# A third scatter epoch for the last two blocks, and node results normalised in place

## The chip, the core and the metric

The kernel runs on one core of one Trainium2 chip. The metric is device time in microseconds (us) for one execution; the median of three runs before the change is 1638.09 us (1637.46 to 1638.39). Engines are named as the profile names them: PE (matrix multiply), PEld (its weight loads), DVE (vector), ACT (scalar), POOL (GpSimd, which here issues the indirect DMAs) and SP (which issues most plain DMAs). "PEclk" is the share of full clock that PE was granted.

## What is computed

A graph layer on 6250 nodes and 206,250 edges, then a residual and a layer norm. Cut to what matters:

```python
msg = concat([x[col], edge_attr], 1)          # col = dst, sorted; row = src, random
h = relu(msg @ W1a.T + b1a) @ W1b.T + b1b
agg = segment_sum(h, row) / max(counts, 1)
z = relu(concat([x, agg]) @ W2a.T + b2a) @ W2b.T + b2b
out = layernorm(x + concat([z, x]) @ Wr.T + br)
```

The hard part is the sum over `row`: the edges come in an order that has nothing to do with their target node.

## The kernel before, in words

**Blocks, bins, tiles.** The edges go through in 124 blocks of 13 columns of 128 edges. The target nodes are 49 bins of 128 nodes. For each bin there is a run of slots in DRAM; 128 slots are a *tile* (128 rows of 130 floats, 66.56 KB). For each block the kernel computes the first layer (PE, line 1355; ACT, line 1358), counts on PE and DVE which slot of its bin each edge gets, and POOL scatters the rows, one indirect DMA per column of 128 edges (`scatter`, line 1395). Blocks 4 to 103 also join part of their edges four to a row in a tensor of their own; from block 104 on there are 13 scatters a block and no joins.

**Epochs and steps.** An epoch is a run of blocks with its own slots. A bin's slots are sized for the worst count it may see (`cap` tiles), and at least `low` tiles are surely full; slots between `low` and `cap` are cleared beforehand by DMAs on ACT's queue (`clear`, line 1443, one every second block, twelve and one for each epoch). Before the change there are two epochs, of 114 and 10 blocks. As the edges come in, *steps* read back the tiles that are full by then: a step is a range of tiles for every bin, cut into *groups* of up to three bins. For each group SP loads the tiles (`read`, line 1457, into a ring of nine buffers), DVE turns the node numbers of the rows into a 0/1 matrix `oh` (line 1486), PE multiplies it with the rows (line 1505), and DVE adds the sum to `part` (line 1565). A read of an epoch's last step waits for the scatters of all blocks of that epoch; a read of an earlier step only for the blocks up to its own.

**Order.** PE, ACT, DVE and SP run in the order in which the program is written; POOL's scatters are placed by a scheduler, and those of up to three neighbouring blocks are interleaved there. Three blocks after a step is full its groups are queued; whatever is queued at the end of the 124 blocks is summed in a loop behind them (`while issued or marked`). The second epoch's first step (one tile a bin, full at block 120) is queued at block 123 and is mostly summed in that loop: 16 groups of three tiles.

**The last step.** The last step of the last epoch is fused with the node stage. Before the change it has 17 groups of three bins with three tiles each (147 tiles). In turn `i` of its loop each engine works on several groups at different depths: `means` and `scaled` of group i-1 (DVE lines 1859 and 1860; ACT, line 1866), `turned` of i-2 (PE, line 1873; ACT, line 1875), `layer` of i-3 (PE, line 1879; DVE, line 1880), `residual` of i-4 (PE, line 1886; DVE, line 1888), `squares` of i-5 (ACT, line 1894), `written` of i-6 (ACT, line 1899; DVE lines 1900 and 1902; output DMA on SP, line 1907), and the tile sums of group i. The residual result `y` stands in a ring of three buffers, its normalised copy `normed` in a ring of two, from which the output DMA reads.

Of the kernel before, what the change touches and what calls it, by code (L numbers as in the profile page):

```python
# [8 lines left out]
F32 = mybir.dt.float32  # L9
# [5 lines left out]
ALU = mybir.AluOpType  # L15
# [3 lines left out]
P = 128  # L19
# [430 lines left out]
NG = 13  # L450
WIN = 60
STEP = 43
EPOCHS = (114, 10)
NEAR = 8
HEAD = 117
FULL = ((3, 6, 9, 12, 14), (1,))
BIG = 2.0**20
LATE = 3
BUFS = 2
RD = 6  # L460
SUMS, TILES = 3, 12
SEG = 9
# [2 lines left out]
RING = 8  # L465
# [14 lines left out]
def order_of(ngr):  # L480


    return [i * STEP % ngr for i in range(ngr)]
# [3 lines left out]
def fast_path(  # L487
# [37 lines left out]
    D, N = xT.shape  # L525
# [3 lines left out]
    NB = N // P + 1  # L529
    NGR = NT // NG  # L530
    REM = N - (NB - 1) * P
    NE = len(EPOCHS)
    W = H + 2
    BLK = NG
# [28 lines left out]
    def by_bin(of_bin, of_rest):  # L563
        return [of_bin] * (NB - 1) + [of_rest]
# [9 lines left out]
    def low_of(b, n, first=0):  # L574
        _, mean, dev = edges_of(b, n, first)
        return max(0, int(mean - dev)) // P
# [21 lines left out]
    epochs, at_blk = [], 0  # L598
    for e, n in enumerate(EPOCHS):
        ep_ = Epoch()  # L600
# [13 lines left out]
        ep_.steps, lo = [], by_bin(0, 0)  # L614
        for t in FULL[e]:
            at = next(k for k in range(n) if low_of(0, k, ep_.first) >= t)
# [9 lines left out]
    qep.first, qep.end = JOIN_FROM, JOIN_TO  # L626
    assert JOIN_TO <= EPOCHS[0]

# [16 lines left out]
    NQ = NB * QSTRIDE  # L645
    NREST = P * NJOIN
    for ep_ in epochs:
        ep_.name, ep_.masked, ep_.stride = "", True, None
    qep.name, qep.masked = "q", False

    PADT = max(c - l for ep_ in epochs[:BUFS] for c, l in zip(ep_.cap, ep_.low))
    PADT = max(PADT, max(c - l for c, l in zip(qep.cap, qep.low)))
    STRIDE = max(max(ep_.cap) for ep_ in epochs) * P
    assert NE == BUFS

    const = ctx.enter_context(tc.tile_pool(name="fconst", bufs=1))
    dram = ctx.enter_context(tc.tile_pool(name="fdram", bufs=1, space=DRAM))
    buffers = [dram.tile([NB * STRIDE, W], F32, name=f"rows{i}") for i in range(BUFS)]
    for e, ep_ in enumerate(epochs):
        ep_.rows = buffers[e % BUFS]  # L660
    qep.rows = dram.tile([(NQ + NREST) * QUAD, W], F32, name="quads")
    relt = dram.tile([NGR, NG * P], BF16, name="relt")
    ytab = dram.tile([NB * P, H], F32, name="ytab")
# [66 lines left out]
    hi = ep.tile([P, NT], BF16, name="hi")  # L730
    lo = ep.tile([P, NT], BF16, name="lo")
    rowidx = ep.tile([P, RING * NG], I32, name="rowidx")
# [10 lines left out]
    nc.vector.tensor_copy(mvs[:, :, H:], ident[:, None, WIDE : WIDE + 2].to_broadcast([P, MV, 2]))  # L743
    padrow = const.tile([P, PADT * W], F32, name="padrow")
    nc.gpsimd.memset(padrow, 0.0)
# [4 lines left out]
    with (  # L750
# [173 lines left out]
        state = {"rt": 0, "bad": 3}  # L924
# [38 lines left out]
        nc.vector.memset(even, FULLQUADS)  # L963
        NBAD = 15 + 5 * NE + 2 * sum(map(len, FULL)) + 2 * len(FULLQ)
        bad = const.tile([P, NBAD], F32, name="bad")
# [115 lines left out]
        def places(k, ps):  # L1081


            t = direct(k) + 1
            if joined(k):
                return ps[:, 0, : 2 * HALF * t].rearrange("p (o b t) -> p o b t", o=1, t=t)
            return ps[:, :, : HALF * t].rearrange("p i (b t) -> p i b t", t=t)
# [94 lines left out]
        def slots(k, ps):  # L1182

            ep_ = epoch_of[k]
            c0 = k * BLK
            at = (k - ep_.first) % SEG * BLK
            if at == 0:
                m = min(ep_.end - k, SEG) * BLK
                state["bin"] = slp1.tile([P, SEG * BLK], F32, name="bin_at")[:, :m]
                nc.vector.tensor_scalar(  # L1190
                    state["bin"], hi[:, c0 : c0 + m], float(STRIDE), -BIG, op0=ALU.mult, op1=ALU.add
                )
            j0 = JOIN * joined(k)
            n = BLK - j0
            v = places(k, ps)
            row = slp.tile([P, T], F32, name="row")[:, :n]
            nc.vector.tensor_reduce(
                row, v[:, :, :, :n].rearrange("p i b t -> p t i b"), axis=mybir.AxisListType.XY, op=ALU.max
            )

            def by_now(t):
                nc.vector.tensor_copy(t.rearrange("p (i b) -> p i b", i=v.shape[1]), v[:, :, :, n])

            nc.vector.scalar_tensor_tensor(
                rowidx[:, k % RING * BLK + j0 : (k % RING + 1) * BLK], row, BIG + STRIDE - 1,
                state["bin"][:, at + j0 : at + BLK], op0=ALU.min, op1=ALU.add,
            )
            if k + 1 == EARLY:
                by_now(early)
                wrong(early, epochs[0].low, ALU.is_gt, slp)  # L1210
            for st in ep_.steps[:-1]:
                if k + 1 == st.at:
                    full = slp1.tile([P, 2 * HALF], F32, name="full")
                    by_now(full)
                    wrong(full, st.hi, ALU.is_lt, slp)
            if k + 1 == ep_.end:
                by_now(ep_.tot)
                if (ep_.end - ep_.first) * BLK > 255:
                    most = slp.tile([P, 2 * HALF], F32, name="most")
                    nc.vector.tensor_scalar(  # L1220
                        most, hads[k][:, :, n], 255.5, None, op0=ALU.is_gt, op1=ALU.add,
                        accum_out=bad[:, state["bad"] :][:, :1],
                    )
                    state["bad"] += 1
# [392 lines left out]


        clears = {5 + 2 * i: (0, i) for i in range(CLEAR)}
        for e in range(1, BUFS):  # L1620
            clears.update({EARLY - 23 + 24 * e + 2 * i: (e, i) for i in range(CLEAR)})
        clears.update({6 + 2 * i: (-1, i) for i in range(CLEAR)})
        assert max(clears) < EPOCHS[0] and 5 + 2 * CLEAR <= EARLY

# [59 lines left out]
        counts = counts_of(0, *bins_of(0))  # L1684
        columns(0)
        slots(0, counts)
        for k, ep_ in enumerate(epoch_of):

# [6 lines left out]
            j0 = JOIN * joined(k)  # L1695
# [101 lines left out]
            if k + 1 < NGR:  # L1797
                slots(k + 1, counts)
# [45 lines left out]
        NF = N // P  # L1844
        with tc.tile_pool(name="nw2", bufs=2) as nw2, tc.tile_pool(name="nw", bufs=3) as nw, tc.tile_pool(
            name="nw1", bufs=1
        ) as nw1:

            class Nodes:

# [31 lines left out]
                def residual(self):  # L1882
                    p3 = hp.tile([P, SUMS, D], F32, name="h_ps")
                    for j in range(self.nb):
                        b = slice((self.b0 + j) * P, (self.b0 + j + 1) * P)
                        nc.tensor.matmul(p3[:, j, :], nq[:, b], wzz_t, start=True, stop=True)
                    y = self.y = nw.tile([P, SUMS, D], F32, name="y")
                    nc.vector.tensor_add(y[:, : self.nb, :], p3[:, : self.nb, :], xr[:, self.bins, :])

                def squares(self):  # L1890
# [5 lines left out]
                def written(self):  # L1896
                    n, b0 = self.nb, self.b0
                    rstd = nw.tile([P, SUMS], F32, name="rstd")
                    nc.scalar.activation(rstd[:, :n], self.ssq[:, :n], AF.Sqrt, bias=eps, scale=1.0 / D)
                    nc.vector.reciprocal(rstd[:, :n], rstd[:, :n])  # L1900
                    y = nw2.tile([P, SUMS, D], F32, name="normed")
                    nc.vector.tensor_tensor(
                        y[:, :n, :], self.y[:, :n, :], rstd[:, :n, None].to_broadcast([P, n, D]), op=ALU.mult
                    )
                    full = min(n, NF - b0)
                    if full > 0:
                        nc.sync.dma_start(
                            out[b0 * P : (b0 + full) * P].rearrange("(b p) f -> p b f", p=P), y[:, :full, :]
                        )
                    if full < n:  # L1910
                        nc.sync.dma_start(out[NF * P :], y[:REM, full, :])
# [112 lines left out]
```

## Time and profile before

| | us |
|---|---|
| median of three runs | 1638.09 |
| profiled execution, its own time | 1640.12 |
| its span, first to last instruction | 1638.2 |
| PE busy | 1436.9 (88%) |
| DVE busy | 1359.4 (83%) |
| POOL busy | 1160.3 (71%) |
| ACT busy | 1102.8 (67%) |
| last scatter starts at | 1555.99 |
| sums of the last step run on PE from, to | 1562.99, 1621.3 |

All positions in time are us from the start of the span of the one profiled execution. Busy shares are means over stages with different limits, so a stage is read from its own rows. On PE each product shows as two records, so "x18" on line 1505 is nine tiles. A timeline row gives start, duration, engine, line, operation, result and operands, and in brackets how long the engine had stood idle and what ended that. In DVE rows that follow at once, the start of the next row is the better measure of what one costs, since the end of one overlaps the start of the next.

### The profile page before, as it was taken

To read this page: it belongs to the slowest core of one execution; us is meant where nothing else is said; L and a number is where in the kernel's file an instruction comes from. 1 tells how busy PE (TensorE), PEld (TensorE's weight loads), DVE (VectorE), ACT (ScalarE), POOL (GpSimd) and SP (SyncE) were. 2 spreads that over 40 slices of the span, in tenths; PEclk is the share of its full clock that TensorE was granted. 3 is DMA by queue.
4 is the path that set the end of the run, shared out by engine and by line. 5 is a ranking of instruction groups with operands and counts; after the bars stand their busy time and mean duration, and the time that the engine had idled before them with its cause. 6 is when DMAs were issued, how large, how long until landed. Compare 5 with 4: busy or idle time off the path is not lost.

```text
span 1638.2 us, 33212 instructions
## 1 busy us (share of the span) xinstructions
PE 1436.9 (88%) x10881; PEld 1306.3 (80%) x10881; DVE 1359.4 (83%) x3176; ACT 1102.8 (67%) x2247; POOL 1160.3 (71%) x1250
## 2 busy tenths in 40 slices
PE   6688888989999999999999999999986998799587
PEld 5577777778888888888888888888876998798476
DVE  7598888887888888999999999999966886776476
ACT  3289999987877777778878788877852344332044
POOL 6777777777777777777777777777776777777700
PEclk9699999999999999999999999999988999999788
DMA  8768888887887988677677667676879999897472
GB/s 208 218 227 288 289 285 293 293 262 240 251 259 227 269 237 246 203 231 216 202 222 217 216 204 235 199 227 194 237 229 342 324 324 290 265 280 241 132 207 78
DMA packets 230179, 393.44 MB, mean 240 GB/s; under 512 B 43205, under 2 KB 164935, under 8 KB 229743
## 3 DMA queue, kind: packets, MB, share of 16 engines
q1 hardware_dynamic: 155629, 224.57, 48.4%
q0 software_dynamic: 48240, 121.28, 21.0%
q10 hardware_dynamic: 26130, 45.38, 7.9%
q8 instruction: 89, 1.46, 0.4%
q14 instruction: 91, 0.75, 0.1%
HBM read 217.82 MB, written 173.25 MB: 239 GB/s over the span
## 4 chain that ended last, share of the span: by engine, by line
PE 55%; ACT 15%; DMA 14%; DVE 8%; issue 4%; POOL 2%; ACTq 1%; SPq 0%; DVEq 0%; POOLq 0%
PE h_ps L1505 23%; PE h_ps L1267 11%; DMA rows<-orow,rowidx 9%; PE h_ps L1355 9%; PE h_ps L1280 5%; ACT rhs L1320 4%; ACT rj L1272 3%; ACT orow L1283 2%; POOL rows L1395 2%; DMA rt<-rows 2%; DVE marks L1235 1%; ACT orow L1358 1%; ACT marks L1240 1%; ACT rhs L1318 1%; PE cnt_ps L1094 1%
## 5 line engine op out<-in xcount | busy, mean ns | idle before, releaser
L1395 POOL DMA_INDIRECT rows<-orow,rowidx x985 | 952.6, 967 | 329.8 <-issue 174.1
L1505 PE MATMUL h_ps<-rt,oh 128*128 128x129 f32 x4036 | 504.0, 280 | 43.8 <-DVE oh L1486 39.4
L1505 PEld LDWEIGHTS h_ps<-rt,oh 128*128 128x128 f32 x4036 | 479.3, 195 | 46.5 <-issue 40.8
L1486 DVE TENSOR_TENSOR oh<-ramp,rt 128x768 f32<-128x768 bf16 (+2 forms) x427 | 317.8, 779 | 46.0 <-DMA rt<-rows 42.3
L1267 PE MATMUL h_ps<-marks,side 128*128 128x512 f32 x1254 | 317.3, 402 | 2.8 <-ACT xr_now L1655 2.2
L1355 PE MATMUL h_ps<-mv,rhs 124*128 124x128 f32 x1970 | 278.3, 287 | 31.6 <-ACT orow L1358 31.5
L1280 PE MATMUL h_ps<-mv,rj 128*128 128x130 f32 x1672 | 234.1, 286 | 72.4 <-ACT orow L1283 45.5
L1280 PEld LDWEIGHTS h_ps<-mv,rj 128*128 128x128 f32 x1672 | 212.8, 193 | 106.2 <-ACT orow L1283 57.6
L1355 PEld LDWEIGHTS h_ps<-mv,rhs 124*128 124x128 f32 x1970 | 249.6, 198 | 35.8 <-ACT orow L1358 33.4
L1267 PEld LDWEIGHTS h_ps<-marks,side 128*128 128x128 f32 x1254 | 229.7, 190 | 48.3 <-ACT xr_now L1655 3.5
L1235 DVE TENSOR_TENSOR marks<-quad_ramp,ramp 128x1024 fp32r<-128x1024 f32 x209 | 250.6, 1203 | 0.0
L1366 POOL DMA_INDIRECT quads<-orow,qidx x209 | 202.3, 968 | 66.1 <-issue 18.4
L1358 ACT ACTIVATE orow<-h_ps 128x384 f32<-128x384 f32 (+1 forms) x287 | 151.4, 536 | 143.5 <-PE h_ps L1355 138.0
L1272 ACT COPY rj<-h_ps 128x512 f32<-128x512 f32 x209 | 119.7, 588 | 77.4 <-PE h_ps L1267 76.8
L1565 DVE TENSOR_TENSOR part<-part,h_ps 128x387 f32<-128x387 f32 (+2 forms) x232 | 113.1, 488 | 68.4 <-PE h_ps L1505 67.6
L1241 ACT ACTIVATE marks<-marks,ones 128x512 fp32r<-128x512 f32 x209 | 150.9, 722 | 6.8
L1283 ACT ACTIVATE orow<-h_ps 128x260 f32<-128x260 f32 x418 | 139.8, 389 | 23.3 <-PE h_ps L1280 19.4
L1240 ACT ACTIVATE marks<-quad_ramp,z_act 128x512 fp32r<-128x512 f32 x209 | 149.4, 715 | 0.0
L1052 DVE TENSOR_TENSOR_SCAN had<-ramp,bins 128x400 bf16<-128x400 bf16 (+1 forms) x124 | 135.0, 1089 | 17.1 <-ACT bins L1073 4.5
L1318 ACT ACTIVATE rhs<-rhs,from_win 60x896 f32<-60x896 bf16 (+1 forms) x116 | 130.5, 1125 | 2.9
L1320 ACT ACTIVATE rhs<-rhs,ones 60x896 f32<-60x896 f32 (+1 forms) x116 | 130.2, 1122 | 2.9
L1346 ACT CAST orow<-lo 128x7 f32<-128x7 bf16 (+1 forms) x124 | 24.2, 195 | 150.9 <-DMA rows<-orow,rowidx 139.1
(189 smaller groups left out, 1471.9 us busy)
## 6 DMA issues: line engine op xcount, KB each, us to landing
rt<-rows SPq DMA_DIRECT2D x145, 390.0 KB
rt<-quads SPq DMA_DIRECT2D x98, 390.0 KB
rhs<-in_edgeT SPq DMA_DIRECT2D x91, 224.0 KB
rt<-rows SPq DMA_DIRECT2D x98, 195.0 KB
enat<-in_edgeJ SPq DMA_DIRECT2D x91, 192.0 KB
rows<-orow,rowidx POOLq DMA_INDIRECT x985
rows<-padrow ACTq DMA_DIRECT2D x12, 1300.0 KB
quads<-padrow ACTq DMA_DIRECT2D x11, 1300.0 KB
```

What stands on the lines that cost most here:

```text
L1235: nc.vector.tensor_tensor(m[:, :n, :], all_q[:, None, :].to_broadcast([P, n, QUAD * P]), z[:, :n, None].to_broadcast([P, n, QUAD * P]), op ...
L1267: nc.tensor.matmul(ps, s[:, p, i * JOIN + t, :], m[:, t, :], start=t + p == 0, stop=t == JOIN - 1 and p == 1,)
L1272: nc.scalar.copy(rj, ps)
L1280: done[k, f"join{i}"] = nc.tensor.matmul(ps[:, j, :], rj[:, (g0 + j) * P : (g0 + j + 1) * P], m, start=True, stop=True).ins.name
L1283: nc.scalar.activation(mrow[:, g0 : g0 + 2, :], ps, AF.Relu)
L1320: nc.scalar.activation(rhs[D:WIDE, :], rhs[D:WIDE, :], AF.Relu, bias=ones[D:WIDE, :1], scale=-1.0)
L1355: done[k, c] = nc.tensor.matmul(ps[:, j, :], rhs[:WIDE, of * P : (of + 1) * P], m[:WIDE, :H], start=True, stop=True).ins.name
L1358: nc.scalar.activation(orow_of(k, k0, n)[:, :, :H], ps[:, :n, :], AF.Relu)
L1366: s = nc.gpsimd.indirect_dma_start(out=qep.rows.rearrange("(q r) f -> q (r f)", r=QUAD), out_offset=bass.IndirectOffsetOnAxis(ap=qidx[:, q ...
L1395: s = nc.gpsimd.indirect_dma_start(out=ep_.rows, out_offset=bass.IndirectOffsetOnAxis(ap=rowidx[:, k % RING * BLK + j : k % RING * BLK + j ...
L1486: nc.vector.tensor_tensor(res[:, at_tile : at_tile + nb * n, :], ramp[:, None, :].to_broadcast([P, nb * n, P]), node[:, :, None].to_broadc ...
L1505: m = nc.tensor.matmul(of_bin(b), oh[:, at_tile, :], rt[:, j * n + t, : H + 1], start=t0 + t == st.lo[b], stop=t0 + t == st.hi[b] - 1,)
```

## The change

Three epochs of 114, 8 and 2 blocks take the place of 114 and 10. Each has its own DRAM tensor and its own number of slots per bin (`ep_.stride`: 2560, 512 and 256 rows; before, 2560 for both). The second epoch's caps are 3 or 4 tiles a bin and the third's 1 or 2. Its clears (twelve and one) come at blocks 55 to 77. In the node stage the normalised result is written over `y`, and `y` has five buffers where `y` and `normed` had three and two.

```diff
-EPOCHS = (114, 10)
+EPOCHS = (114, 8, 2)
-FULL = ((3, 6, 9, 12, 14), (1,))
+FULL = ((3, 6, 9, 12, 14), (1,), ())
...
-        ep_.name, ep_.masked, ep_.stride = "", True, None
+        ep_.name, ep_.masked, ep_.stride = "", True, max(ep_.cap) * P
...
-    STRIDE = max(max(ep_.cap) for ep_ in epochs) * P
-    assert NE == BUFS
...
-    buffers = [dram.tile([NB * STRIDE, W], F32, name=f"rows{i}") for i in range(BUFS)]
     for e, ep_ in enumerate(epochs):
-        ep_.rows = buffers[e % BUFS]
+        ep_.rows = dram.tile([NB * ep_.stride, W], F32, name=f"rows{e}")
...
-        for e in range(1, BUFS):
+        for e in range(1, NE):
             clears.update({EARLY - 23 + 24 * e + 2 * i: (e, i) for i in range(CLEAR)})
...
-                    y = self.y = nw.tile([P, SUMS, D], F32, name="y")
+                    y = self.y = nw5.tile([P, SUMS, D], F32, name="y")
...
-                    y = nw2.tile([P, SUMS, D], F32, name="normed")
+                    y = self.y
                     nc.vector.tensor_tensor(
-                        y[:, :n, :], self.y[:, :n, :], rstd[:, :n, None].to_broadcast([P, n, D]), op=ALU.mult
+                        y[:, :n, :], y[:, :n, :], rstd[:, :n, None].to_broadcast([P, n, D]), op=ALU.mult
                     )
```

What it moves, on SP, behind the 16 reads of the second epoch's first step. In these rows `rows_65` is the second epoch's tensor, `rows_66` the third's, and "128x3x260" is three bins of two tiles. Before, the first rows of the last step, which reads three tiles a bin, in pairs of a two-bin and a one-bin read:

```order
L1457 DMA rt<-rows_65 128x3x130 x16
L1457 DMA rt<-rows_65 128x2x390
L1457 DMA rt<-rows_65 128x390
L1457 DMA rt<-rows_65 128x2x390
L1457 DMA rt<-rows_65 128x390
```

After, from the same place, the first and the last rows of what stands there:

```order
L1453 DMA rt<-rows_65 128x3x130 x16
L1453 DMA rt<-rows_65 128x3x260 x3
L1453 DMA rt<-rows_65 128x2x260
L1453 DMA rt<-rows_65 128x390
L1453 DMA rt<-rows_65 128x260
```

```order
L1453 DMA rt<-rows_65 128x2x260
L1453 DMA rt<-rows_65 128x390
L1453 DMA rt<-rows_66 128x3x130 x5
L1453 DMA rt<-rows_66 128x260
L1453 DMA rt<-rows_66 128x2x130
```

The second epoch's rest is now a step of its own, 17 groups in 27 reads with 106 tiles, summed in the loop behind the blocks; the node stage follows with the third epoch's 17 groups in 19 reads with 51 tiles.

On POOL, the end of the scatters. Buffers `orow_141` and `orow_142` hold the rows of blocks 120 and 121, `orow_143` and `orow_144` those of blocks 122 and 123. The order is that of before, where all of them went to `rows_65`; after, the last rows read:

```order
L1391 DMA rows_65<-orow_141,rowidx 25088x130
L1391 DMA rows_66<-orow_143,rowidx 12544x130 x3
L1391 DMA rows_66<-orow_144,rowidx 12544x130 x2
L1391 DMA rows_65<-orow_142,rowidx 25088x130
L1391 DMA rows_66<-orow_143,rowidx 12544x130
L1391 DMA rows_66<-orow_144,rowidx 12544x130
L1391 DMA rows_65<-orow_142,rowidx 25088x130 x2
L1391 DMA rows_66<-orow_143,rowidx 12544x130
L1391 DMA rows_66<-orow_144,rowidx 12544x130
L1391 DMA rows_65<-orow_142,rowidx 25088x130
L1391 DMA rows_66<-orow_144,rowidx 12544x130 x7
```

Behind these stand four more to `rows_66`. The last scatter of the second epoch is thus the twelfth from the end.

On DVE, one turn of the node stage's loop, before:

```order
L1565 TENSOR_TENSOR part<-part,h_ps 128x387
L1859 TENSOR_SCALAR rc<-part 128x3
L1860 RECIPROCAL rc<-rc 128x3
L1900 RECIPROCAL rstd<-rstd 128x3
L1902 TENSOR_TENSOR normed<-y,rstd 128x192
L1888 TENSOR_TENSOR y<-h_ps,xr 128x192
L1880 TENSOR_TENSOR x_late<-x_late,h_ps 128x384
L1486 TENSOR_TENSOR oh<-ramp,rt 128x768
L1486 TENSOR_TENSOR oh<-ramp,rt 128x384
```

After:

```order
L1561 TENSOR_TENSOR part<-part,h_ps 128x387
L1855 TENSOR_SCALAR rc<-part 128x3
L1856 RECIPROCAL rc<-rc 128x3
L1896 RECIPROCAL rstd<-rstd 128x3
L1898 TENSOR_TENSOR y<-y,rstd 128x192
L1884 TENSOR_TENSOR y<-h_ps,xr 128x192
L1876 TENSOR_TENSOR x_late<-x_late,h_ps 128x384
L1482 TENSOR_TENSOR oh<-ramp,rt 128x384
```

One of the two `oh` rows has gone from the turn, and the normalisation writes to what it reads. PE's tile sums in a turn go from nine tiles to three.

More of the change, by code (lines that the diff above doesn't have):

```diff
@@ L452 @@
 STEP = 43
-EPOCHS = (114, 10)
+EPOCHS = (114, 8, 2)
 NEAR = 8
 HEAD = 117
-FULL = ((3, 6, 9, 12, 14), (1,))
+FULL = ((3, 6, 9, 12, 14), (1,), ())
 BIG = 2.0**20
 LATE = 3
-BUFS = 2
 RD = 6
@@ L647, in fast_path @@
     for ep_ in epochs:
-        ep_.name, ep_.masked, ep_.stride = "", True, None
+        ep_.name, ep_.masked, ep_.stride = "", True, max(ep_.cap) * P
     qep.name, qep.masked = "q", False
-    PADT = max(c - l for ep_ in epochs[:BUFS] for c, l in zip(ep_.cap, ep_.low))
+    PADT = max(c - l for ep_ in epochs for c, l in zip(ep_.cap, ep_.low))
     PADT = max(PADT, max(c - l for c, l in zip(qep.cap, qep.low)))
-    STRIDE = max(max(ep_.cap) for ep_ in epochs) * P
-    assert NE == BUFS
     const = ctx.enter_context(tc.tile_pool(name="fconst", bufs=1))
     dram = ctx.enter_context(tc.tile_pool(name="fdram", bufs=1, space=DRAM))
-    buffers = [dram.tile([NB * STRIDE, W], F32, name=f"rows{i}") for i in range(BUFS)]
     for e, ep_ in enumerate(epochs):
-        ep_.rows = buffers[e % BUFS]
+        ep_.rows = dram.tile([NB * ep_.stride, W], F32, name=f"rows{e}")
     qep.rows = dram.tile([(NQ + NREST) * QUAD, W], F32, name="quads")
@@ L1190, in slots @@
                 nc.vector.tensor_scalar(
-                    state["bin"], hi[:, c0 : c0 + m], float(STRIDE), -BIG, op0=ALU.mult, op1=ALU.add
+                    state["bin"], hi[:, c0 : c0 + m], float(ep_.stride), -BIG, op0=ALU.mult, op1=ALU.add
                 )
@@ L1204, in slots @@
             nc.vector.scalar_tensor_tensor(
-                rowidx[:, k % RING * BLK + j0 : (k % RING + 1) * BLK], row, BIG + STRIDE - 1,
+                rowidx[:, k % RING * BLK + j0 : (k % RING + 1) * BLK], row, BIG + ep_.stride - 1,
                 state["bin"][:, at + j0 : at + BLK], op0=ALU.min, op1=ALU.add,
@@ L1846, in fast_path @@
             name="nw1", bufs=1
-        ) as nw1:
+        ) as nw1, tc.tile_pool(name="nw5", bufs=5) as nw5:
             class Nodes:
```

## Prediction

> **What bounds the kernel now.** The change leaves the first 114 blocks alone but for some clears, so I read the end first: the busy time by stage, from the windows view (columns: PE, PEld, DVE, ACT, POOL busy with counts, PEclk, DMA share, GB/s).
>
> ```profile
> span 1638.2 us, 33212 instructions
> 1520.00:1560.00 40.00, 16.02 (x118) 13.88 (x116) 15.25 (x33) 0.00 (x0) 28.10 (x30) 0.75 0.38 107
> 1580.00:1600.00 20.00, 20.00 (x163) 18.43 (x162) 18.32 (x49) 14.47 (x66) 0.00 (x0) 1.00 0.63 175
> 1598.66:1609.60 10.94, 10.94 (x89) 10.00 (x89) 10.12 (x28) 6.77 (x34) 0.00 (x0) 1.00 0.59 161
> ```
>
> From 1520 to 1560 PE is busy for 16 of 40 us while POOL works through the last scatters; from 1580 on PE is never idle. So there is a hole ahead of the node stage, and a node stage that PE bounds. The chain that ended last says where the hole ends and what one turn of the node stage costs (start, us, what):
>
> ```profile
> 1542.11 2.44 DMA rows<-orow,rowidx
> ...
> 1555.99 2.29 DMA rows<-orow,rowidx
> ...
> 1558.46 3.38 DMA rt<-rows
> ...
> 1561.93 0.97 DVE oh L1486
> ...
> 1562.99 4.22 PE h_ps L1505 x18
> ...
> 1587.69 2.01 PE h_ps L1505 x18
> 1589.70 0.61 PE h_ps L1886 x6
> 1590.32 0.70 PE h_ps L1879 x2
> 1591.02 0.33 PE h_ps L1873 x3
> ...
> 1616.94 2.02 PE h_ps L1505 x18
> ```
>
> The last scatter lands at 1558.3, the last step's first read needs 3.5 us until DVE can start, and the first nine tiles are summed at 1567.21. A turn takes PE 2.01 + 0.61 + 0.70 + 0.33 = 3.65 us, of which nine tiles take 2.01, 0.223 each. The sixteenth group is summed at 1618.96, so fifteen turns take 51.75 us.
>
> **The change, part by part.**
>
> *The rest of the second epoch (106 tiles) moves into the hole.* It may start when its own last scatter has landed. By POOL's order that is the twelfth scatter from the end. POOL issues one every 1.262 us ((1555.99 - 1542.11) / 11), so it is the one of the chain's first row, down at 1544.55: the reads get 14 us of the hole, not all of it. As before, DVE starts some 3.5 us after that, at 1548.0. What the 17 groups cost DVE stands in the timeline of the preceding sums:
>
> ```profile
> 1505.22 1.81 DVE L1486 TENSOR_TENSOR oh<-ramp,rt 128x768 f32<-128x768 bf16 x2
> ...
> 1533.36 0.55 DVE L1565 TENSOR_TENSOR part<-part,h_ps 128x387 f32<-128x387 f32 x1
> 1533.82 0.55 DVE L1486 TENSOR_TENSOR oh<-ramp,rt 128x384 f32<-128x384 bf16 x1
> 1534.29 0.55 DVE L1565 TENSOR_TENSOR part<-part,h_ps 128x387 f32<-128x387 f32 x1
> ...
> 1535.22 1.69 DVE L1565 TENSOR_TENSOR part<-part,h_ps 128x387 f32<-128x387 f32 x3
> ```
>
> An add costs 0.46 and an `oh` of three tiles 0.47 from start to start, one of six tiles 0.905; a straight line gives 0.147 a tile and 0.025 a read. So 106 x 0.147 + 27 x 0.025 + 17 x 0.46 = 24.1 us on DVE. PE's 106 x 0.223 = 23.7 us lie beside it. But PE has stood still from 1536 on and starts cold: before, its first nine tiles took 4.22 us instead of 2.01 (the chain), in a window with PEclk 0.58 (the second row of the next fence), so 2.2 us more. The Trainium skill, "TensorE: Matmul & The Clock Gate", Part 1, states that a PE idle for some 3.4 us falls to half clock and needs about 3.4 busy us to come back. By that the loss is an estimated 1.7 us, and the sum 0.5 us shorter; the row shows a longer loss, and I take the row. Behind the last `oh` come the last sum and its add, 0.67 + 0.46 us. The rest is done at 1548.0 + 24.1 + 2.2 + 1.1 = 1575.4.
>
> Can the reads keep up? From the DMA view, 1518 to 1528 and 1562 to 1568 (packets, MB, share):
>
> ```profile
> 1516.00:1530.00 14.00, 13.85 (x113) 12.88 (x112) 10.46 (x23) 0.00 (x0) 10.64 (x12) 1.00 0.95 254
> 1562.00:1568.00 6.00, 5.01 (x27) 5.04 (x28) 3.50 (x6) 0.00 (x0) 0.00 (x0) 0.58 1.03 360
> q1 hardware_dynamic: 3977, 1.98, 78.1%
> rt<-rows SPq DMA_DIRECT2D x11, 195.0 KB
> ...
> q1 hardware_dynamic: 1494, 2.16, 102.9%
> ```
>
> Reads of one tile a bin (packets of 520 bytes) take 0.781 x 16 x 10 us / 3977 = 31 ns a packet, those of three tiles 66 ns. The rest has two tiles a bin, between them: about 49 ns, so 106 tiles in 53 x 128 packets keep 16 engines for 20.8 us. That is under DVE's 24.1, so DMA costs nothing here; if that cover is gone, see the second rival. The same 1516 row has POOL at its pace (12 scatters in 14 us) beside a busy DVE and 95% DMA, so the last scatters do not slip.
>
> *The third epoch's first group.* Its rows have long landed by 1575.4. One `oh` (0.47) and three tiles (0.67) put the first sum at 1576.5, against 1567.21: **+9.3 us**.
>
> *The turns of the node stage.* They lose six tiles on PE (3.65 - 1.34 = 2.32 us left, with three tiles at 0.67) and one `oh` on DVE. One turn on DVE:
>
> ```profile
> 1615.33 0.56 DVE L1565 TENSOR_TENSOR part<-part,h_ps 128x387 f32<-128x387 f32 x1 [0.17 <-PE h_ps L1505]
> 1615.92 0.17 DVE L1859 TENSOR_SCALAR rc<-part 128x3 f32<-128x3 f32 x1
> 1616.13 0.18 DVE L1860 RECIPROCAL rc<-rc 128x3 f32<-128x3 f32 x1
> 1616.22 0.15 DVE L1900 RECIPROCAL rstd<-rstd 128x3 f32<-128x3 f32 x1
> 1616.40 0.36 DVE L1902 TENSOR_TENSOR normed<-y,rstd 128x192 f32<-128x192 f32 x1
> 1616.68 0.35 DVE L1888 TENSOR_TENSOR y<-h_ps,xr 128x192 f32<-128x192 f32 x1
> 1616.94 0.55 DVE L1880 TENSOR_TENSOR x_late<-x_late,h_ps 128x384 f32<-128x384 f32 x1
> 1617.41 0.55 DVE L1486 TENSOR_TENSOR oh<-ramp,rt 128x384 f32<-128x384 bf16 x1
> ...
> 1581.22 1.28 ACT L1899 ACT_TABLE_LOAD   x1
> ```
>
> From 1615.33 to 1617.41 are 2.08 us, and the `oh` adds 0.47: 2.55 us a turn. ACT has 6.77 us in the three turns from 1598.66, 2.26 each. So **DVE takes PE's place as the bound**, at 2.55 us. The first turns have less: two without `x_late`, `y`, `rstd` and `normed` (1.36 each by the same starts), one with `x_late` (1.83), two with `y` too (2.09 each), then ten full ones; and ACT's table load, hidden before in a turn of 3.65 us, falls in a turn of 2.1 and is counted in full, 1.28. Together 2.72 + 1.83 + 4.18 + 25.5 + 1.28 = 35.5 us against 51.75: **-16.2 us**. Bounds for the turn: 2.32 (PE's) and 3.65 (as before); 2.55 is the sum of rows that follow at once.
>
> *Five buffers, in place.* The multiplication reads and writes the same shapes, so it costs its 0.28 us still. It no longer waits for an output to land, which it does twice at the end:
>
> ```profile
> 1629.26 0.36 DVE L1902 TENSOR_TENSOR normed<-y,rstd 128x192 f32<-128x192 f32 x1 [0.21 <-DMA out_dram<-normed]
> ...
> 1631.83 0.36 DVE L1902 TENSOR_TENSOR normed<-y,rstd 128x192 f32<-128x192 f32 x1 [2.13 <-DMA out_dram<-normed]
> ```
>
> Both lie on the path: **-2.3 us**. The wait moves to the writer of `y`, three turns after the output is issued, 7.6 us at 2.55. The chain has the wait for an output at
>
> ```profile
> 1628.24 3.50 DMA out_dram<-normed
> ```
>
> 3.5 us, so nothing is late there.
>
> *Clears.* Thirteen more DMAs on ACT's queue at blocks 55 to 77, and smaller ones for the second epoch.
>
> ```profile
> L1443 ACTq DMA_DIRECT2D rows<-padrow x26: 338/366/672, 87.5 to 629.4; - x26
> 480.00:800.00 320.00, 299.05 (x2295) 271.26 (x2294) 285.49 (x690) 254.40 (x505) 235.25 (x245) 1.00 0.77 231
> ```
>
> An issue takes ACT 0.366 us: 0 to 4.8 us in all. There ACT is busy for 254 of 320 us and PE, at 299, is nearer to being the bound, so I take **+1.0**. The added DVE rows at blocks 120 to 123 (a memset, a copy, a check) fall where DVE waits for PE: nothing.
>
> *Sum:* 9.3 - 16.2 - 2.3 + 1.0 = -8.2 us. The profiled execution took 1640.12 (its span and 1.9 us around it) and would take 1631.9; the median of the runs lies 2.0 lower, so 1638.09 - 8.2 = **1629.9**.
>
> **The rivals.**
>
> 1. *The rest waits for the last scatter of all.* If its reads are let go only at 1558.4 and not at 1544.6, all that follows is 13.8 us later: 1643.7, slower than before. The point from which it decides: a start after 1552.8 eats the gain, one after 1556 makes it slower by more than 0.2%. For it: before, the last step's first read follows the last scatter in the chain. Against it: the second epoch's one-tile reads landed (11 of them from 1518 to 1528) while scatters to the same tensor went on.
>
> 2. *The rest is bound by its reads.* Those 11 reads moved 198 GB/s beside the scatters, 0.336 us a tile. At that rate 106 tiles take 35.6 us instead of the 26 that DVE and the cold PE need, some 9 us more: 1639. For it: 95% DMA share in that window. Against it: packets twice as long, and no scatters after 1558. The Trainium skill, "DMA: Bandwidth & Descriptors", "Why small descriptors are slow (HBM only)", gives a fixed overhead of about three cycles a packet, which makes two-tile packets hardly dearer per byte than three-tile ones and speaks against this rival; the two rows above (31 and 66 ns for a third and all of the bytes) show a larger one.
>
> 3. *The turns do not reach DVE's sum.* With the engines nearly level (2.55, 2.32, 2.26) each waits for the other; at 3.0 us a turn the ten full turns give back 4.5 us, and the shorter ones 1.5: 1636.
>
> 4. *The rest starts earlier,* at 1527, if all of blocks 120 and 121 were scattered ahead of 122. Some 14 us better: 1616. POOL's order speaks against it.
>
> **How the numbers follow.** Forecast 1629.9 (0.70; its own range 1623 to 1636, from 2 to 3 us either way in the rest's start and pace, 1.5 in the turns, 0 to 4.8 in the clears); rival 1: 0.06; rival 2: 0.12; rival 3: 0.07; rival 4: 0.05. The range 1623 to 1640 takes in rivals 2 and 3. A measurement of this kernel can tell about 0.2% (3.3 us) from no change. Faster by more than that is below 1634.8: nearly all of the forecast, rival 4 and a part of rival 3, 0.77. Slower is above 1641.4: rival 1, 0.06. Between: 0.17.
>
> **What would show it.** The first `rt` read of the rest issued near 1544.6, in step with the twelfth scatter from the end; DVE without idle from 1548 to 1575; the first three-tile sum of the node stage near 1576; turns of 2.55 us with PE waiting for `oh` or for DVE's results; no output DMA named as releaser of the normalisation; and positions up to block 113 within some 2 us of before. Wrong would be: reads released with the last scatter (rival 1), DVE waiting for `rt` throughout the rest (rival 2), turns near 3 us (rival 3), or the blocks' own pace changed by more than the clears can explain.

## The result, and the profile after

The changed kernel takes 1633.93 us (median of 12 runs, 1630.50 to 1640.22) against 1640.88 us for the kernel before (12 runs, 1637.41 to 1644.56): a ratio of 0.9961, 95% interval 0.9946 to 0.9976, so 6.4 us (2.5 to either side) faster. Its profiled execution took 1632.16 us, its span is 1630.3.

The windows of the changed kernel (columns as before: PE, PEld, DVE, ACT, POOL busy with counts, PEclk, DMA share, GB/s):

```profile
span 1630.3 us, 33371 instructions
1520.00:1560.00 40.00, 26.38 (x193) 24.27 (x192) 26.46 (x52) 0.00 (x0) 25.35 (x27) 0.83 0.69 206
1544.00:1574.00 30.00, 26.84 (x220) 26.71 (x221) 26.29 (x48) 0.00 (x0) 7.14 (x8) 0.89 0.96 298
1580.00:1600.00 20.00, 19.27 (x134) 16.35 (x133) 17.41 (x56) 16.72 (x75) 0.00 (x0) 0.97 0.35 85
```

From 1520 to 1560 PE is busy for 26 us instead of 16: the hole is partly filled. From 1580 on PE has pauses where it had none. The timeline shows what starts the filling:

```profile
1538.43 0.96 POOL L1391 DMA_INDIRECT rows<-orow,rowidx  x1 [0.30 <-DMA rows<-orow,rowidx]
...
1540.92 43.09 SPq L1453 DMA_DIRECT2D rt<-rows  x41
...
1545.21 0.96 DVE L1482 TENSOR_TENSOR oh<-ramp,rt 128x768 f32<-128x768 bf16 x1 [12.81 <-DMA rt<-rows]
...
1546.27 25.92 PE L1501 MATMUL h_ps<-rt,oh 128*128 128x129 f32 x212 [13.33 <-DVE oh L1482]
...
1552.32 0.96 POOL L1391 DMA_INDIRECT rows<-orow,rowidx  x1 [0.30 <-issue]
```

The first row is the twelfth scatter from the end. SP issues the rest's first read 2.5 us behind its start, DVE takes it up 4.3 us later, and PE needs 25.9 us for the 106 tiles (212 records), most of it behind the last scatter. Then the chain (start, us, what) shows the node stage:

```profile
1573.08 0.92 PE h_ps L1501 x6
...
1589.61 0.48 DVE part L1561
...
1592.14 0.48 DVE part L1561
...
1594.67 0.47 DVE part L1561
...
1612.30 0.51 DVE part L1561
...
1623.29 0.23 DVE y L1898
```

The adds to `part` stand 2.53 us apart and lie on the chain: DVE sets the turn. Since whole executions differ by 3 or 4 us whatever the kernel, I compare all traces by their distance from the start of their last scatter (us; "first rc" is DVE's first `rc` of the node stage, 0.6 behind its first sum):

| kernel (chip) | rest's first `oh` | first rc | 16th rc | last normalisation ends | span ends |
|---|---|---|---|---|---|
| before | | 11.84 | 63.59 | 76.54 | 82.21 |
| after | -7.11 | 22.30 | 60.52 | 71.20 | 77.98 |
| e8_before (8) | | 16.27 | 68.02 | 81.30 | 87.32 |
| e2_buffers (8) | | 16.24 | 67.99 | 78.68 | 85.98 |
| e1_epochs (8) | | 38.25 | 74.83 | 87.67 | 93.50 |
| e4_wait_last (8) | | 38.37 | 76.61 | 87.30 | 93.91 |
| e9_after (14) | | 39.15 | 75.75 | 86.44 | 93.35 |
| e6_warm (14) | | 39.79 | 77.08 | 87.77 | 94.05 |
| e5_order (14) | | 47.45 | 84.06 | 94.75 | 101.29 |
| g1_order (13) | | 45.62 | 82.23 | 92.93 | 100.08 |
| f1_light_before (6) | | 11.96 | 63.80 | 75.93 | |
| f2_light_after (6) | -12.44 | 16.58 | 53.16 | 63.87 | |
| f3_light_order (6) | | 7.43 | 44.01 | 54.70 | |
| g2_order (6) | -18.32 | 9.53 | 46.11 | 56.80 | 63.11 |

So the tail shrank by 82.21 - 77.98 = 4.2 us. The other 3.7 us between the two spans are a last scatter that came at 1552.32 instead of 1555.99; the experiments ask whether that is the change's.

The chips matter here: on chip 6 and in the measurement above, whose chip isn't known, the kernel before takes 1638 to 1641 us at a mean granted clock near 0.96; on chips 8, 13 and 14 it takes 2118 to 2151 us at 0.87. Ratios are always to the kernel before on the same chip.

### The profile page after: what moved, and what is told of

The parts are those of the page before. It is cut to its first block, busy times and chain, and to the rows that moved or that the text cites. A ratio compares the mean times of both kernels' runs of the same rounds, so it can differ in the third digit from the quotient of the medians.

```text
span 1630.3 us, 33371 instructions
## 1 busy us (share of the span) xinstructions
PE 1442.6 (88%) x10901; PEld 1309.7 (80%) x10901; DVE 1369.7 (84%) x3210; ACT 1103.3 (68%) x2246; POOL 1160.6 (71%) x1268
## 4 chain that ended last, share of the span: by engine, by line
PE 56%; ACT 17%; DMA 12%; DVE 8%; issue 4%; POOL 2%; SPq 0%; ACTq 0%; DVEq 0%; POOLq 0%
PE h_ps L1501 24%; PE h_ps L1263 11%; PE h_ps L1351 9%; DMA rows<-orow,rowidx 8%; PE h_ps L1276 5%; ACT rhs L1316 4%; ACT rj L1268 3%; ACT orow L1279 2%; POOL rows L1391 2%; DMA rt<-rows 2%; ACT orow L1354 2%; ACT marks L1236 2%; ACT rhs L1314 1%; DVE marks L1231 1%; PE cnt_ps L1090 1%
## 5 line engine op out<-in xcount | busy, mean ns | idle before, releaser
L1482 DVE TENSOR_TENSOR oh<-ramp,rt 128x768 f32<-128x768 bf16 (+3 forms) x440 | 321.3, 763 | 30.5 <-DMA rt<-rows 27.0
L1561 DVE TENSOR_TENSOR part<-part,h_ps 128x387 f32<-128x387 f32 (+2 forms) x249 | 122.2, 491 | 66.8 <-PE h_ps L1501 65.3
```

Of the source, the lines that this page charges most:

```text
L1482: nc.vector.tensor_tensor(res[:, at_tile : at_tile + nb * n, :], ramp[:, None, :].to_broadcast([P, nb * n, P]), node[:, :, None].to_broadc ...
```

## The experiments

**The parts alone, and the start of the rest.** Epochs without the new rings:

```diff
-                    y = self.y = nw5.tile([P, SUMS, D], F32, name="y")
+                    y = self.y = nw.tile([P, SUMS, D], F32, name="y")
...
-                    y = self.y
+                    y = nw2.tile([P, SUMS, D], F32, name="normed")
```

> The three epochs alone, with the old rings (y of three, normed of two). Theory A (the rest of the second epoch fills the scatter hole and the node stage becomes DVE-bound; the buffers only clear the drain): the turns stay at 2.53 us and the sixteenth sum of the node stage stays where the change has it (some 60 us after the start of the last scatter), while the drain behind it goes back from 11.0 to 13.3 us, with an output DMA named as releaser; 2.3 us slower than the whole change, so some 4 us (0.25%) faster than before. Rival B (the buffers carry most of the gain): about as slow as before, with waits for outputs inside the turns, near 3 us each.

The rings without the epochs (the same lines the other way round, in the kernel before):

> The five in-place buffers alone, with two epochs. Theory A: turns stay at 3.65 us and PE-bound, the first sum of the node stage stays 11.2 us behind the start of the last scatter, the drain takes 11.0 us instead of 13.3: 2.3 us (0.14%) faster than before. Rival B: faster by 5 us or more. For the 3.5 us that the changed kernel was ahead from 57 us on: if the third tensor and its addresses cause it, the blocks start here where they start in before; if it is chance, anywhere within some 4 us of both.

The whole change with a later start of the rest:

```diff
+            if st is epochs[1].steps[-1]:
+                of += [t for j in (122, 123) for t in range(j * BLK, (j + 1) * BLK)]
             for t in of:
```

> The whole change, but the reads of the rest of the second epoch also wait for the scatters of blocks 122 and 123. Theory A (the gain hangs on when the rest may start): the first of these reads goes out with the last scatter's landing, 13.9 us later than in the changed kernel, and all behind it is later by as much, less what a wholly idle DMA gives back (up to 1 us): tail from the last scatter's start 91 us instead of 78, so some 13 us slower than the changed kernel and 6 us (0.4%) slower than before. Rival (the node stage's faster turns are worth having wherever the rest stands): no slower than before.

And the kernel before, unchanged:

> The kernel before once more, for a second profile of its blocks. If the 3.5 us by which the changed kernel's blocks ran ahead are chance of one execution, its blocks start at places that differ from the first profile by as much as 2 to 4 us, and the lead stems from the same transfers near 40 to 57 us; if they are the change's, the blocks start where they did, within 0.5 us.

Measured on chip 8: e1_epochs 2126.22 us, ratio 1.0058 (1.0022 to 1.0093); e2_buffers 2118.55, 1.0006 (0.9972 to 1.0040); e4_wait_last 2132.98, 1.0077 (1.0034 to 1.0120); e8_before 2123.58 in its one run. **The epochs alone are slower than before here**, which neither theory had: turns are 2.53 us as expected, but the first rc stands at 38 instead of 22, and e4's extra wait changes nothing (first rc 38.37 against 38.25). The reason is in e8_before already. PE's largest wait (us in total, times, longest), and PE's rows ahead of the last scatter at 2034.48:

```profile
PE h_ps L1505 <- issue: 129.4, 140, 7.5
```

```profile
2018.26 1.07 PE L1505 MATMUL h_ps<-rt,oh 128*128 128x129 f32 x3 [1.03 <-issue]
2020.36 0.37 PE L1505 MATMUL h_ps<-rt,oh 128*128 128x129 f32 x1 [1.03 <-issue]
2021.06 0.38 PE L1505 MATMUL h_ps<-rt,oh 128*128 128x129 f32 x1 [0.32 <-issue]
2022.46 0.38 PE L1505 MATMUL h_ps<-rt,oh 128*128 128x129 f32 x1 [1.02 <-issue]
...
2030.19 16.12 PE L1505 MATMUL h_ps<-rt,oh 128*128 128x129 f32 x100 [0.60 <-issue]
```

PE stands still again and again with nothing that the trace names ("issue"; why it does, no run shows), and is still summing the second epoch's first step when the last scatter is out. There is no hole: the rest is queued behind those sums, so its 24 us come on top whenever it is let go. That is why e4 can't price rival 1 here; on a chip with a hole it wasn't tried. What the two kernels have in common with the first pair still shows: in e1_epochs the drain waits for an output as before,

```profile
2116.68 0.36 DVE L1898 TENSOR_TENSOR normed<-y,rstd 128x192 f32<-128x192 f32 x1 [2.09 <-DMA out_dram<-normed]
```

and nowhere else, and from the 16th rc to the last normalisation it takes 12.8 us against 10.7 in e2_buffers (13.3 in e8_before). So rival B, that the buffers carry the gain, falls: they touch the drain alone.

**The changed kernel beside the kernel before, idle products, another order of the scatters.** Three kernels on chip 14. The changed kernel once more:

> The changed kernel once more, beside the kernel before on the same chip. Theory A with its condition (the change pays only if PE has done with the sums of the second epoch's first step before that epoch's last scatter lands): on a chip with a granted clock near 0.96, 0.2 to 0.6% faster than before, the tail behind the last scatter's start 78 us against 82; on one near 0.87, where the tail of the three epochs alone took 93.5 us against 87.3, 91 us against 87 and so 0.1 to 0.3% slower. Rival (the gain came from a start that was 3.5 us ahead in the first 60 us): on either chip the same ratio.

Products that nobody reads in the first four turns:

```diff
                 if i < n_last:
                     on_way.append(Nodes(sum_next(NGR)))
+                if i < 4:
+                    for _ in range(3):
+                        nc.tensor.matmul(cnt[:, 1, :P], ident, ident, start=True, stop=True)
```

> The whole change with three idle products of 128x128 (0.22 us each, into a bank that nobody reads) behind the sums of the first four turns of the node stage. If the half clock of the fourth turn (PEclk 0.50 from 1578 to 1580, the layer's product 1.65 us instead of 0.86) comes from PE standing still for much of 1572 to 1578, the clock stays at 1.00 and the turn takes 2.4 us instead of 4.2: 1 to 2 us faster than the changed kernel. Rival (the clock falls there for another reason): turns as before, up to 1 us slower for the added products.

The scatters of the last four blocks without the waits that interleave them:

```diff
+            if k >= 120:
+                pace = {}
             for j in range(j0, BLK):
```

> The whole change, but the scatters of blocks 120 to 123 no longer wait for the products of later blocks, so that POOL's order puts all 26 scatters of blocks 120 and 121 ahead of the 26 of blocks 122 and 123: the last scatter of the second epoch is the twenty-seventh from the end instead of the twelfth. Theory A (the rest's start sets the gain): where PE is granted nearly full clock, the first reads of the rest follow at once behind those of the second epoch's first step, about 5 us earlier than in the changed kernel, DVE and PE go on without a pause and without the half clock, and the first sum of the node stage stands some 9 us behind the start of the last scatter instead of 21: 8 to 13 us faster than the changed kernel. Rival (the rest is bound by its reads beside the scatters, 0.336 us a tile): the rest takes 36 us and the gain is 3 us at most. On a chip with the lower clock (0.87) the sums of the second epoch's first step end behind the last scatter anyway, so there it should change nothing.

Measured: e9_after 2160.93 us, ratio 1.0060 (1.0029 to 1.0090); e6_warm 2156.27, 1.0008 (0.9972 to 1.0044); e5_order 2158.34, 1.0031 (0.9996 to 1.0067). The whole change is slower than before on such a chip, by more than I expected. By the table, e9_after's tail is 6.0 us longer than that of e8_before, on another chip (93.35 against 87.32): its first rc comes 22.9 us later, its turns and drain give back 17.7, its end costs 0.9. The interval, 6 to 19 us, may hold more than that; what else there is stays open. That rest, on a PE that comes to it warm:

```profile
2095.25 23.91 PE L1501 MATMUL h_ps<-rt,oh 128*128 128x129 f32 x212 [0.42 <-PE h_ps L1501]
```

```profile
2090.00:2120.00 30.00, 28.62 (x244) 27.48 (x242) 29.45 (x58) 0.00 (x0) 0.00 (x0) 1.00 0.92 277
```

DVE is busy for 29.45 of 30 us. The new order of scatters doesn't help here, as expected; its distances from the last scatter are longer, as that scatter no longer waits for PE and goes out earlier relative to it.

e6 went at one row of the first profile. In what follows a turn is counted by the rc that ends it, so the fourth turn lies between the third rc and the fourth. After's PE in its first turns, and the stretches at half clock in after and in e4_wait_last (granted clock: third number from the end):

```profile
1575.55 0.91 PE L1869 MATMUL h_ps<-ident,agg 128*128 128x128 f32 x3 [0.89 <-ACT agg L1862]
1576.30 0.84 PE L1501 MATMUL h_ps<-rt,oh 128*128 128x129 f32 x6
1577.75 1.65 PE L1875 MATMUL h_ps<-aT,wam_t 128*128 128x384 f32 x2 [0.61 <-ACT aT L1871]
1579.19 0.84 PE L1869 MATMUL h_ps<-ident,agg 128*128 128x128 f32 x3
1579.84 1.48 PE L1501 MATMUL h_ps<-rt,oh 128*128 128x129 f32 x6
```

```profile
1577.75:1581.16 3.41, 3.41 (x12) 2.69 (x13) 1.37 (x4) 1.46 (x4) 0.00 (x0) 0.50 0.16 39
```

```profile
2063.05:2066.46 3.41, 3.41 (x15) 2.85 (x14) 1.51 (x4) 1.46 (x4) 0.00 (x0) 0.50 0.13 34
```

PE runs at half clock for 3.4 us though it had not stood still for more than 0.9 us since the rest began; the fourth turn takes 4.24 us. In e4_wait_last it takes 3.97 and the fifth 0.3 too long, in the other seven kernels with three epochs and without the idle products the fourth takes 2.59 to 2.60. So it strikes by chance, in two of nine executions, and costs 1.65 us both times (38.2 us from the first rc to the 16th, against 36.6). With the idle products the clock stayed at 1.00, but in one execution that shows little; they also cost 0.7 us in the fifth turn (3.12 against 2.44). Whether they prevent the half clock stays open. The Trainium skill, "TensorE: Matmul & The Clock Gate", Part 1, has the clock set by PE's activity in a free-running window of some 3.4 us. The 3.41 us of each stretch agree with that, and so does that the same instructions meet it in one execution and not in the next. Its rule of one idle window alone doesn't give the fall: PE was busy for 3.17 of the 5.50 us from 1572.20 on, with no idle time above 0.9 us.

**PE put in time by leaving out products.** To get the hole back on whatever chip, three kernels multiply only the first tile of each bin in late steps:

```diff
                     for t in range(n):
+                        light = st.at >= 104 and st.epoch in (qep, epochs[0])
+                        if light and t0 + t != st.lo[b]:
+                            at_tile += 1
+                            continue
...
-                            start=t0 + t == st.lo[b], stop=t0 + t == st.hi[b] - 1,
+                            start=t0 + t == st.lo[b], stop=light or t0 + t == st.hi[b] - 1,
```

With these products missing, the program goes on into its general path behind the node stage (6.9 ms in all), so only positions up to the last normalisation are read.

> The kernel before, relieved on PE: of the steps that are full at block 104 or later in the first epoch and among the joined rows, only the first tile of each bin is multiplied (some 650 products fewer in blocks 108 to 122, so its output isn't the reference's; reads, DVE's matrices and scatters stay). Its use is to put PE in time for the end of the scatters on a chip whose PE is slow. Expected: PE waits for the last scatter again, the first sum of the node stage ends some 11 us behind its start as in the first profile (16.3 without the relief here), and the tail from its start takes 81 to 83 us.

> The changed kernel with the same relief (the same products left out). Theory A (the change pays when PE has done with the first step of the second epoch before that epoch's last scatter lands, and costs when not): the reads of the rest go out 11 to 12 us ahead of the last scatter's start again, instead of 2 to 4 us behind it, the first rc of the node stage stands at 22 us instead of 38 to 39, and the tail takes 76 to 78 us, 4 to 6 us less than that of the relieved kernel before. Rival (this chip's transfers or engines, not PE's lateness, make the change slower here): the tail stays at 90 us or more, longer than that of the relieved kernel before.

> The changed kernel with the same relief, and with the scatters of blocks 120 and 121 all ahead of those of 122 and 123. Theory A (with PE in time, the rest's start sets the gain): the reads of the rest follow the twenty-seventh scatter from the end, some 30 us ahead of the last one's start, the rest is summed before the last scatter lands, the first rc of the node stage stands 9 to 11 us behind the last scatter's start, and the tail takes 64 to 67 us, 10 to 13 us less than with the old order. Rival (the reads beside the scatters are so slow, 0.336 us a tile, that the early start is lost): first rc at 14 us or later, or scatters stretched from their 1.26 us.

They came to chip 6, where PE isn't late even without the relief. Windows from 1540 to 1560 of f1_light_before, then of f2_light_after, then of f3_light_order (and its 20 us ahead):

```profile
1540.00:1560.00 20.00, 0.00 (x0) 0.00 (x0) 0.00 (x0) 0.00 (x0) 11.79 (x13) 0.50 0.22 66
```

```profile
1540.00:1560.00 20.00, 16.12 (x130) 16.15 (x131) 16.10 (x29) 0.00 (x0) 12.45 (x13) 0.82 1.00 320
```

```profile
1520.00:1540.00 20.00, 19.08 (x144) 16.89 (x143) 19.80 (x40) 0.00 (x0) 15.12 (x17) 1.00 1.00 314
1540.00:1560.00 20.00, 16.88 (x147) 16.36 (x146) 16.68 (x32) 0.00 (x0) 11.83 (x13) 1.00 0.78 249
```

In f1 PE and DVE do nothing at all in the hole; its last normalisation ends at 75.93, as in the kernel before (76.54). In f2 the work starts inside the hole, and it ends at 63.87, 12.1 us sooner than f1; the full kernel gained 5.3 to the same point (76.54 - 71.20), and I had expected 4 to 6. Between the two changed kernels, 71.20 and 63.87, lie 7.3 us, and two things make them. The products left out also move POOL's order: here the last scatter of the second epoch is the sixteenth from the end, not the twelfth, so its reads go out 5.0 us sooner (4 x 1.262). The first `oh` stands at -12.44 instead of -7.11, 5.3 sooner, and the first rc at 16.58 instead of 22.30, 5.7 sooner: **the start of the rest passes through to the node stage, nearly us for us.** And the half clock didn't strike (1.65). In f3 the rest is done when the last scatter lands; first rc at 7.43, end at 54.70. The rival with slow reads falls: the first rc is well ahead of its 14 us, and at a DMA share of 1.00 POOL kept its 1.26 us a scatter. No run on chips 8, 13 or 14 took PE's lateness away, so that this lateness makes the change slower there is read from their traces, not shown by an experiment.

**The new order, nothing left out.** The kernel of e5_order ran on two more chips.

> The kernel with the scatters of blocks 120 and 121 ahead of those of 122 and 123 and nothing left out, once more. Theory A, for a chip on which PE is granted about 0.96 (on one with 0.87 it repeats what was seen there): PE ends the second epoch's first step some 19 us ahead of the last scatter's start, the rest follows without a pause, DVE needs 24 us for it, so the first rc of the node stage stands 7.5 to 10 us behind the last scatter's start (22.3 in the changed kernel, 7.4 in the relieved kernel with this order), and the last normalisation ends 55 to 58 us behind it (71.2 in the changed kernel): 12 to 16 us faster than the changed kernel, a ratio of 0.985 to 0.990 to the kernel before. Rival (the later scatters of blocks 120 and 121, freed of their wait, get in PE's or ACT's way, or the reads beside them are too slow): less than 6 us faster than the changed kernel.

Measured on chip 13: 2133.43 us, ratio 1.0057 (1.0023 to 1.0091); PE was late again (first rc 45.62).

> The same kernel as in the run before (the scatters of blocks 120 and 121 ahead of those of 122 and 123, nothing left out), sent again because three of the four chips so far granted PE 0.87. Where it is granted about 0.96, theory A and its rival expect what they did there: a ratio of 0.985 to 0.990 to the kernel before, first rc 7.5 to 10 us behind the last scatter's start, against less than 6 us gained on the changed kernel. On one with 0.87, a third time a ratio near 1.004.

Measured on chip 6: **1620.49 us against 1639.84, ratio 0.9884 (0.9866 to 0.9902)**, 19 us faster than before and 13 faster than the changed kernel by the ratios. One window of it and two pieces of its chain:

```profile
1524.00:1550.00 26.00, 25.29 (x201) 23.18 (x200) 26.00 (x52) 0.00 (x0) 19.75 (x21) 1.00 1.00 298
```

```profile
1537.92 18.91 PE h_ps L1503 x166
1556.83 0.09 issue
1556.92 5.39 PE h_ps L1503 x46
```

DVE is busy for 26.00 of 26 us across what was the hole, PE never falls to half clock (1.00), and POOL's 21 scatters keep their pace. PE's 212 records take 24.4 us from end to end against 25.9 in the changed kernel. The first `oh` of the rest comes 11.2 us sooner than in the changed kernel (-18.32 against -7.11) and the first rc 12.8 us sooner, about the sum of that and the 1.5 that a warm PE saves. First rc 9.53 and last normalisation 56.80 are where theory A had them.

**The 3.7 us ahead of the tail.** The same scan of a late block (DVE) in the kernel before, the changed one, f1_light_before, f2_light_after and g2_order; what was left out of f1 and f2 comes later than this:

```profile
1091.85 0.99 DVE L1052 TENSOR_TENSOR_SCAN had<-ramp,bins 128x400 bf16<-128x400 bf16 x1
```

```profile
1088.35 0.99 DVE L1048 TENSOR_TENSOR_SCAN had<-ramp,bins 128x400 bf16<-128x400 bf16 x1
```

```profile
1090.39 0.99 DVE L1052 TENSOR_TENSOR_SCAN had<-ramp,bins 128x400 bf16<-128x400 bf16 x1
```

```profile
1090.45 0.99 DVE L1048 TENSOR_TENSOR_SCAN had<-ramp,bins 128x400 bf16<-128x400 bf16 x1
```

```profile
1091.35 0.99 DVE L1048 TENSOR_TENSOR_SCAN had<-ramp,bins 128x400 bf16<-128x400 bf16 x1
```

The code of before stands at 1091.85 and 1090.39, that of the change at 1088.35, 1090.45 and 1091.35. Two executions with the change's code stand among those of before, so a lead of 3.5 us is one execution's and not the change's; one of 1 us couldn't be told from chance here. e8_before, meant for this question, ran on a chip whose positions can't be compared.

## Why the prediction came out as it did

The forecast was 1629.9 us, 8.2 us faster; measured were 6.4 (3.9 to 8.9). The mechanism was right: the rest goes into the hole, starts with the twelfth scatter from the end, and DVE bounds the node stage. That the two profiled spans differ by 7.9, nearly the forecast, is partly luck: 3.7 of it is the chance lead, for which one of the prediction's own signs (positions up to block 113 within some 2 us of before) failed, and the steps of the forecast for the tail (-9.2 without the clears) gave -4.2. The chance half clock is 1.65 of the 5.0 that are missing; without it the tail would be an estimated 5.9 shorter (4.2 + 1.65), near the measured 6.4. Step by step, by the table:

- *The rest's start and length, +9.3 for the first sum.* It came 10.5 later (22.30 - 11.84). The reads went out as forecast; DVE had its first tile 4.3 us behind, not 3.5. From there to the last add it took 27.3, against the 27.4 forecast. The loss to a cold PE was sized rightly at 2.2, from the first nine tiles of before. After's PE ran its first 4.17 us of the rest at half clock and was never idle from there on:

```profile
1546.27:1550.44 4.17, 4.17 (x19) 4.17 (x20) 3.95 (x7) 0.00 (x0) 3.26 (x4) 0.50 1.07 383
1550.45:1572.00 21.55, 21.55 (x195) 21.54 (x193) 19.95 (x38) 0.00 (x0) 2.22 (x3) 1.00 0.95 284
```

  Its 212 records took 25.9 us; at 2.01 us for 18 they take 23.7. So in the changed kernel PE, not DVE, bounds the rest. The forecast put PE's loss on top of DVE's 24.1 and left out the 1.1 us from DVE's first tile to PE's first product; that the two nearly cancel is luck. Against the rests that found PE warm, which DVE bounds, the cold start cost 1.5 (24.4 in g2_order) to 2.0 (23.9 in e9_after). The Trainium skill, "TensorE: Matmul & The Clock Gate", Part 1, by which I had estimated 1.7, states some 3.4 busy us until the clock comes back. The trace shows 4.17, so here that estimate was too low for PE's own loss.
- *The turns, -16.2.* They gave -13.5 (38.2 instead of 35.5 for fifteen). This is **the term that was mis-sized**. The full turn is 2.53 against 2.55, so adding up DVE's rows was right. The error is in the first five turns behind the first rc, where I also added up DVE's rows, 8.7 us. Without the half clock they take 10.6 (1.32, 1.83, 2.60, 2.44 and 2.41 in g2_order). While the pipeline fills, a turn isn't set by DVE's busy time alone but by one group's way through `scaled`, `turned` and `layer`, and DVE waits for it. The chain of g2_order in its third and fourth turn, and DVE's wait there:

```profile
1566.46 0.99 ACT agg L1864 x3
1567.44 0.37 ACT aT L1873
...
1567.86 0.91 PE h_ps L1877 x2
```

```profile
1568.81 0.55 DVE L1878 TENSOR_TENSOR x_late<-x_late,h_ps 128x384 f32<-128x384 f32 x1 [0.56 <-PE h_ps L1877]
```

  The half clock added 1.65 in the profiled execution. The table load cost less than counted: its turn takes 3.25, 0.6 under 2.55 + 1.28.
- *Five buffers, -2.3.* In the drain it is -2.3 (10.68 against 12.95 from the 16th rc to the last normalisation). But the end behind it grew from 5.7 to 6.8, and from 6.0 in e8_before to 7.3 in e2_buffers: without the waits the last outputs come to SP close together. SP's last row in before, then its last two in after:

```profile
1632.69 0.31 SPq L1911 DMA_DIRECT2D out_dram<-normed  x1
```

```profile
1618.86 4.93 SPq L1903 DMA_DIRECT2D out_dram<-y  x5
1623.88 0.70 SPq L1907 DMA_DIRECT2D out_dram<-y  x1
```

  The last issue ends 1.06 us behind DVE's last row (1623.52), against 0.47 before (1632.69 + 0.31 against 1632.53). That is 0.6 of the 1.1 by which the end grew; the other 0.5 lie behind the last issue, and why is open. So the buffers are worth 1.2 to 1.3, and I had not followed the wait to the queue behind it.
- *Clears, +1.0.* Nothing to be seen: at the scan above, no execution with the change's code stands later than 1091.85, where the first of before stands.
- *The rivals.* Rivals 2 and 3 did not come: at a DMA share of 0.96 the rest was still bound by PE, and the full turns reached DVE's sum. Rival 4, all of blocks 120 and 121 scattered first, was priced at 1616, 22 us under before; g2_order measured 1620.49, 19 under its 1639.84. Rival 1's outcome, a rest behind the last scatter, does come, but through a door that the prediction didn't name: on chips 8, 13 and 14 PE is late. The prediction took it as a property of the kernel that PE stands still from 1536 on. It is one of the kernel on a chip where PE keeps up, as on chip 6.

## What to carry to other kernels

Work moved into an idle stretch pays only while the engine that does it gets there in time: ask what happens if that engine is late by the length of the stretch. When a wait names a group of transfers, look at where the scheduler put the last of them: setting the second epoch's last scatter fifteen places earlier was worth twice the change itself on chip 6, and nothing that could be told on chips 13 and 14. Summing an engine's rows gives the full turn of a pipeline to 1%, but not the turns that fill it; for those, follow one item through all engines.

## What the runs showed of the hardware

- One core, one program, 30% between chips: 1638 to 1640 us on chip 6, 2118 to 2151 on 8, 13 and 14. In e8_before PE waits 129 us for "issue" on line 1505 alone, where the first profile's largest wait on any line is 45 us (for ACT), and it has stretches in which single products start 0.7, 1.4 or 2.1 us apart. The cause is open.
- PE fell to half clock for 3.4 us without an idle time above 0.9 us in the 5.5 us ahead, in two of nine executions.
- POOL's scatters kept 1.26 us each while the DMA engines showed a share of 1.00 and DVE was never idle (g2_order, 1524 to 1550).
